# Range check in parts, the copy of an accumulator on two engines, and a new order of convolution products in an attention and convolution kernel

## The chip, the cores and the metric

The kernel runs on one core of a Trainium2 chip. The metric is the time on the device in microseconds (us), from the median of the runs shown. A profile of one execution is given beside it; its span is the stretch between the first and the last recorded instruction, and its own time is a little longer.

In the profile PE is TensorE's matmul stream, PEld its stream of weight loads, DVE is VectorE, ACT is ScalarE, POOL is GpSimd and SP is SyncE, which issues most DMA transfers. An L with a number is a line of the kernel before.

## The reference, cut to what matters

Two layers are computed on `x` of shape (8, 64, 64, 64). The first is attention over the 4096 pixels of each image, with means taken off queries and keys and a second, unary softmax:

```python
sim = jnp.einsum('bcn,bcm->bnm', q - q_mean, k - k_mean) / scale
out = jnp.einsum('bnm,bcm->bcn', jax.nn.softmax(sim, axis=2), v)
unary = jax.nn.softmax(jnp.einsum('bc,bcm->bm', q_mean, k - k_mean), axis=-1)
x = x + out + jnp.einsum('bcm,bm->bc', v, unary)[:, :, None]
```

The second takes signs of `x`, convolves them with binarized weights of sizes 1, 3 and 5 (each followed by a batch norm), sums the three, and gates the sum:

```python
s = sum(qconv_bn(x, move_k, w_k, ...) for k in (1, 3, 5))
gate = jax.nn.sigmoid(grouped_linear(jnp.mean(s, axis=(2, 3))))
return s * gate[:, :, None, None] + x
```

## The kernel before, in words

Two images lie side by side on the 128 partitions, so there are `n_pairs` = 4 pairs. The 4096 pixels of a pair are cut into `NQ` = 8 query blocks of 512 columns: 32 blocks in all, numbered g from 0 to 31. A block has 32 steps j. In each step TensorE makes the scores of 128 keys against 512 queries for both images (`ps`, L474, eight float32 matmuls on quadrants of 64x64), ScalarE takes their exponential (`e`, L485), TensorE multiplies it with the values into the accumulator `acc` (L493, eight matmuls), and VectorE adds `e` into `es` (L508) for the denominators. The scores of step j+1 are issued ahead of the product of step j.

`attend` writes the order of all this out by hand. `plan(g)` says which further work is put behind which step. At step 0 of a block stand:

- `weighted_out` of the block before: ScalarE copies `acc`, 128 x 1024 values in two PSUM banks, into the tile `o` (L515). `added` (L582) later adds the two halves of it on VectorE.
- `send` and `gather`: transfers that re-lay `es` for the division.
- `mix_rows`: convolution products of the block three before (L703, with the 1x1 convolution at L785) and, in front of them, the projections of the queries of the next block (`pq`, L460), which VectorE (L467) and ScalarE (L468) turn into `q`.

Within `mix_rows` two sequences run side by side on the two row halves of TensorE's array. One has the query projections, the ten "S" products of the 5x5 convolution, the 1x1 convolution and the twelve products `three` of the 3x3 convolution (A, B, S and D, three each). The other has the projections and the "A", "B" and "D" products of the 5x5 convolution. Their lengths are given in units and the two are merged by these. When the 1x1 convolution is done, ScalarE's `begin_rows` (L729) reads it. When the twelve 3x3 products are done, ScalarE's `hold_rows` (L734) copies them out as `es_z`. When all is done, VectorE's `add_rows` follows (L744, L750).

PSUM has three pools: `ps_s` with two slots of two banks for the scores and the 5x5 products, `ps_a` with one slot of two banks, and `ps_m` with two single banks. The one slot of `ps_a` is taken in turn by `acc` of a block, by the 3x3 products `z3` of `mix_rows`, and by `acc` of the next block. So the first 3x3 product follows the copy of the old `acc`, and the first matmul of the new `acc` follows `hold_rows`.

A range check guards the result: each reciprocal that the softmax uses must lie between 1e-20 and 1e20. `check` has ScalarE take signs of the value against both limits and add them up into a column of the tile `fit`. At the end VectorE adds `fit` up and compares (L1162, L1163), TensorE sums over the partitions (`pb`, L1165), VectorE casts the count to an integer (`good`, L1167), each engine loads it into a register (L1168), and `tc.If` (L1171) jumps over a slow path that is taken only if a check failed. All that stands after `attend` in the text and is placed by a scheduler.

The tail of `attend`, from L1098, handles the last block. It is cut into 320 and 192 columns (`parts`, `halves`). Its reciprocals are made on VectorE (L576), `finish` (L586, L587), signs on ScalarE (L613, L619), then the last two of three direct convolutions, `mix` of rows 6 to 11 and 11 to 16 (L785, with the results on ScalarE at L805 and on VectorE at L809). Then come the check of all 512 reciprocals (L418), `gate_mean` (L815), `gate` (a matmul L819, an exponential L821, L822, L823), a diagonal matrix of the gate (L1127), and the eight results: two through TensorE (`pre`, L1130), ScalarE's copy (L1131) and ScalarE's DMA queue (L1132), six through VectorE (L827) and SP's queue (L828).

Of the kernel before, what the change touches and what calls it, by code (L numbers as in the profile page):

```python
# [18 lines left out]
F32 = mybir.dt.float32  # L19
BF16 = mybir.dt.bfloat16  # L20
I32 = mybir.dt.int32
AF = mybir.ActivationFunctionType
ALU = mybir.AluOpType
AX = mybir.AxisListType
PSUM = bass.MemoryType.PSUM

P = 128
# [4 lines left out]
QB = 512  # L32
NQ = N // QB
# [11 lines left out]
def conv_seq_kernel(ctx, tc, x, wq, wk, wv, vecs, w1, w3, w5, wtap, gw, out):  # L45
    nc = tc.nc
    n_pairs = x.shape[0] * x.shape[1] // P
# [4 lines left out]
    cp = ctx.enter_context(tc.tile_pool(name="const", bufs=1))  # L52
# [3 lines left out]
    fp = ctx.enter_context(tc.tile_pool(name="fp", bufs=1))  # L56
    sm = ctx.enter_context(tc.tile_pool(name="small", bufs=2))
# [5 lines left out]
    def m_tile(name):  # L63
        return ps_m.tile([P, QB], F32, tag="m", name=name)
# [12 lines left out]
    gw_s = cp.tile([P, P], F32, tag="gw", name="gw_s")  # L77
# [28 lines left out]
    ones = cp.tile([P, P], F32, tag="ones", name="ones")  # L106
# [5 lines left out]

    rec = cp.tile([P, 8], F32, tag="rec", name="rec")

    fit = cp.tile([P, 2, n_pairs * (NQ + 1)], F32, tag="fit", name="fit")
    lim = cp.tile([P, 3], F32, tag="lim", name="lim")
    nc.vector.memset(lim[:, 0:1], -LOW)
    nc.vector.memset(lim[:, 1:2], HIGH)
# [138 lines left out]
    class Pair:  # L257
# [152 lines left out]
        def check(self, r, i, sides=(0, 1)):  # L410

            w = r.shape[-1]
            for side in sides:
                if w < QB:
                    junk = self.tile(sm, "ck", f"{i}_{side}", (P, 8), BF16)
                else:
                    junk = self.tile(fp, "rc", f"ck_{i}_{side}", dtype=BF16)
                nc.scalar.activation(  # L418
                    junk[:, 0:w],
                    r,  # L420
                    AF.Sign,
                    bias=lim[:, side : side + 1],
                    scale=1.0 - 2.0 * side,
                    accum_out=fit[:, side, i : i + 1],
                )
# [84 lines left out]
        def weighted_out(self, qb, parts=(slice(0, QB),)):  # L510

            acc = self.acc[qb]
            self.acc[qb] = self.tile(fp, "o", qb, (P, 2, QB))
            for c in parts:
                nc.scalar.copy(self.acc[qb][:, :, c], acc[:, :, c])  # L515

# [59 lines left out]
        def added(self, qb, cols=slice(0, QB)):  # L578
            if cols.start == 0:
                self.x2[qb] = self.tile(bp, "x2", qb)  # L580
            acc = self.acc[qb]
            nc.vector.tensor_tensor(self.x2[qb][:, cols], acc[:, 0, cols], acc[:, 1, cols], ALU.add)  # L582

        def finish(self, qb, cols=slice(0, QB)):
            x2 = self.x2[qb][:, cols]
# [229 lines left out]
            nc.vector.tensor_reduce(self.ga, self.gap[:, 0 : self.n_gaps], AX.X, ALU.add)  # L815

        def gate(self):
            pg = m_tile(f"pg_{self.name}")
            nc.tensor.matmul(pg[:, 0:1], gw_s, self.ga, start=True, stop=True)  # L819
            self.gt = self.tile(sm, "gt", 0, (P, 1))  # L820
            nc.scalar.activation(self.gt, pg[:, 0:1], AF.Exp, bias=ngb, scale=-1.0 / N)  # L821
            nc.vector.tensor_scalar(self.gt, self.gt, 1.0, None, ALU.add)  # L822
            nc.vector.reciprocal(self.gt, self.gt)  # L823
# [57 lines left out]
    def mix_rows(q, c):  # L881


        seqs = [[], []]
        if q is not None:
            for h in range(2):
                seqs[h].append((("q",), 0, 2.0))
        if c is not None:
            p, (r0, _, y) = c
            qb = r0 // ROWS  # L890

            def products(k, name):
                return [((k, name), i, 0.5) for i in range(n_products(k, name))]

            S = products(5, "S")
            three = [t for name in "ABSD" for t in products(3, name)]
            seqs[0] += S[:8] + [((1,), 0, 1.0)] + three + S[8:]
            seqs[1] += products(5, "A") + products(5, "B") + products(5, "D")
        order = []
        for h, seq in enumerate(seqs):  # L900
            at = 0.0
            for t in seq:
                order += [(at, h, b, t) for b in (h, 1 - h)]
                at += t[2]
        order.sort(key=lambda o: o[0:2])
        if q is not None:
            q[0].query_tiles(q[1])
        z, left = {}, {}
        for o in order:
            left[o[3][0]] = left.get(o[3][0], 0) + 1  # L910
        half = [slice(0, QB // 2), slice(QB // 2, QB)]
        for _, h, b, (n, i, _) in order:
            if n == ("q",):
                q[0].split_queries(q[1], b, h)
            else:
                if n not in z:
                    name = f"{p.name}_{qb}_{n[0]}"
                    if n == (1,):
                        z[n] = m_tile(f"z{name}")
                    elif n == (5, "D"):  # L920
                        z[n] = m_tile(f"z{name}d")[:, half[0]]
                    elif n[0] == 3:
                        z3 = ps_a.tile([P, 2, QB], F32, tag="acc", name=f"z{name}")
                        for j, m in enumerate("ABSD"):
                            z[3, m] = z3[:, j // 2, half[j % 2]]
                    else:
                        t = score_banks(f"z{name}")
                        z[5, "S"], z[5, "A"], z[5, "B"] = t[0][:, half[0]], t[1][:, half[0]], t[1][:, half[1]]
                if n == (1,):
                    p.conv_tap((r0, ROWS, y), [[z[n]]], b, 0, 0, 0, True, True)  # L930
                else:
                    p.row_product(z[n], b, *n, i, r0)
            left[n] -= 1
            if left[n] == 0 and n == ("q",):
                q[0].split_queries_out(q[1])
            elif left[n] == 0 and n == (1,):
                p.begin_rows(qb, z[n])
            elif left[n] == 0 and n == (3, "D"):
                p.hold_rows(qb, z3)
        if c is not None:  # L940
            p.add_rows(qb, z[5, "A"], z[5, "B"], z[5, "S"])
            p.z5d = z[5, "D"]
# [21 lines left out]
    def attend(pairs):  # L964
        pending = None
        n_blocks = n_pairs * NQ
# [114 lines left out]
        for g in range(n_blocks):  # L1081
            pr, qb = divmod(g, NQ)
            at = plan(g)
            p = pairs[pr]
# [13 lines left out]
        p, b = pairs[-1], NQ - 1  # L1098
# [14 lines left out]
        for (r0, r1), cols in zip(parts, halves):  # L1113
            if r0 > 0:
                p.reciprocals_wide(b, slice(cols.start + P, cols.stop))
                p.finish(b, cols)
            for n in (2, 1):
                p.signs_wide(b, n, r0, r1, None)
                p.copy_signs(b, n, r0, r1, (nc.vector.tensor_copy, nc.gpsimd.tensor_copy))
            p.signs(b, r0, r1, nc.gpsimd.tensor_copy)  # L1120
        mix(None, (p, p.joint_rows(6, 11)), one_bank, score_banks)
        mix(None, (p, p.joint_rows(11, 16)), one_bank, score_banks)
        p.check(p.r[b], n_blocks - 1)
        p.gate_mean()
        p.gate()
        diag_g = sm.tile([P, P], F32, tag="diag_g", bufs=1, name="diag_g")
        nc.vector.tensor_scalar(diag_g, ident, p.gt, None, ALU.mult)  # L1127
        rows_p = rows_of(n_pairs - 1)
        for i in range(2):
            nc.tensor.matmul(pre[:, i, :], diag_g, p.s[i], start=False, stop=True)  # L1130
            nc.scalar.copy(p.s[i], pre[:, i, :])  # L1131
            nc.scalar.dma_start(out=of[rows_p, bass.ts(i, QB)], in_=p.s[i])  # L1132
        for i in range(2, NQ):
            p.store(i, rows_p)

    with tc.manual_schedule():
        first = Pair("0", xt)
        warm(6)
        projection()
        warm(4)  # L1140
        first.mean_part(0, quarters[0])
        vectors()
        first.mean_part(1, quarters[1], True)
        first.mean_part(2, quarters[2])
        for c in range(2):
            first.mean_part(3 + c, slice(N * (6 + c) // 8, N * (7 + c) // 8), c == 1)
        first.query_tiles(0, score_banks)
        for b in range(2):
            first.queries(0, b)
        load_weights()  # L1150
        warm(18)
        first.mean_sum(5)
        first.mean_scores()
        first.mean_scores_out()
        first.queries_out(0)
        key_bias()
        first.value_weights()
        attend([first] + [None] * (n_pairs - 1))


    nb_ = sm.tile([P, 1], F32, tag="nb", name="nb")
    nc.vector.tensor_reduce(nb_, fit, AX.XY, ALU.add)  # L1162
    nc.vector.tensor_scalar(nb_, nb_, n_pairs * (16.0 * NQ + 2.0) - 16.0 + 2 * QB, None, ALU.is_equal)  # L1163
    pb = m_tile("pb")
    nc.tensor.matmul(pb[:, 0:1], ones, nb_, start=True, stop=True)  # L1165
    good = sm.tile([P, 1], I32, tag="good", name="good")
    nc.vector.tensor_copy(good, pb[:, 0:1])  # L1167
    n_good = nc.values_load(good[0:1, 0:1])  # L1168


    with tc.If(n_good < P):  # L1171
# [117 lines left out]
```

## Time and profile before

| What | Value |
|---|---|
| Median of 3 runs | 1933.31 us (1933.23 to 1934.18) |
| Profiled execution, its own time | 1934.02 us |
| Its span | 1931.8 us |
| TensorE matmuls busy | 1914.2 us, 99% of the span |
| VectorE busy | 1594.1 us, 83% |
| ScalarE busy | 1274.0 us, 66% |
| TensorE clock granted | 1.0 up to 1922.25 us, 0.5 after it |
| ScalarE's copies of `acc` (L515, 1024 columns) | 31, mean 1006 ns |
| `hold_rows` (L734) | 29, mean 1114 ns |

The page that these come from gives busy times by engine, the chain of work that ended last, and groups of instructions by line with the mean time of one and the idle time before it. An engine at 99% can still lose time: matmuls overlap, so start times of neighbours tell more than the busy share.

### The profile page before, as it was taken

What the parts mean: (1) busy time and instruction counts of PE and PEld (TensorE: products, weight loads), DVE (VectorE), ACT (ScalarE), POOL (GpSimd) and SP (SyncE); (2) the same over time, 40 slices, a digit from 0 to 9 for tenths busy, and PEclk for the clock granted to TensorE, in tenths of its full rate; (3) what the DMA queues carried; (4) which work ended last, traced back from release to release, by engine and by line L of the source; (5) the groups of instructions that cost most, each with busy time, mean ns of one, the idle gap of its engine ahead of it and who ended that gap; (6) DMA issues with size and microseconds to landing.
All of it is one profiled execution on the core that took longest, in us unless ns stands there. A gap on an engine that the chain in (4) does not pass through costs nothing.

```text
span 1931.8 us, 48355 instructions
## 1 busy us (share of the span) xinstructions
PE 1914.2 (99%) x20848; PEld 754.9 (39%) x20848; DVE 1594.1 (83%) x2066; ACT 1274.0 (66%) x1523; POOL 5.9 (0%) x26
## 2 busy tenths in 40 slices
PE   9999999999999999999999999999999999999997
PEld 4333343343333333343433333433443333333334
DVE  6878888889887888888888888898887888877876
ACT  5667766666666766666666676666666666666663
POOL 0000000000000000000000000000000000000000
PEclk9999999999999999999999999999999999999999
DMA  3021110110112110101101211011011011111111
GB/s 101 31 70 29 28 40 32 40 35 16 40 35 80 56 51 27 41 32 40 35 16 40 84 53 57 28 29 40 32 40 35 16 56 50 49 39 37 25 35 46
DMA packets 58998, 80.58 MB, mean 42 GB/s; under 512 B 15628, under 2 KB 40600, under 8 KB 58648
## 3 DMA queue, kind: packets, MB, share of 16 engines
q1 hardware_dynamic: 58024, 76.22, 12.9%
q8 instruction: 165, 2.70, 0.6%
q10 hardware_dynamic: 720, 1.18, 0.2%
q14 instruction: 57, 0.47, 0.1%
q0 software_dynamic: 32, 0.01, 0.0%
HBM read 39.27 MB, written 24.77 MB: 33 GB/s over the span
## 4 chain that ended last, share of the span: by engine, by line
PE 97%; DVE 1%; ACT 1%; DMA 0%; issue 0%; SPq 0%; DVEq 0%
PE ps L474 46%; PE acc L493 45%; PE z L703 4%; PE pv L313 1%; PE pq L460 1%; PE z L785 1%; ACT e L485 0%; DMA x<-in_x 0%; DVE es L508 0%; PE warm L155 0%; DVE r L576 0%; PE z_5d L703 0%; DMA out<-sb 0%; ACT o L515 0%; ACT rc_ck L418 0%
## 5 line engine op out<-in xcount | busy, mean ns | idle before, releaser
L485 ACT ACTIVATE e<-ps 128x1024 f32<-128x1024 f32 x1024 | 1049.7, 1025 | 597.8 <-PE ps L474 576.8
L508 DVE TENSOR_TENSOR es<-es,e 128x1024 f32<-128x1024 f32 x960 | 1171.2, 1220 | 187.6 <-ACT e L485 158.2
L474 PE MATMUL ps<-q,x 64*64 64x512 f32 x8192 | 1069.5, 590 | 0.9 <-DVE kb L165 0.9
L493 PE MATMUL acc<-e,v 64*64 64x512 f32 x8192 | 1065.2, 590 | 0.6 <-ACT e L485 0.3
L493 PEld LDWEIGHTS acc<-e,v 64*64 64x64 f32 x8192 | 307.6, 131 | 577.8 <-ACT e L485 305.9
L474 PEld LDWEIGHTS ps<-q,x 64*64 64x64 f32 x8192 | 312.2, 133 | 528.9 <-issue 278.0
L703 PE MATMUL z<-e,wt 64*64 64x256 bf16 x754 | 69.3, 270 | 0.1
L703 PE MATMUL z<-ec,wt 64*64 64x256 bf16 x754 | 69.4, 270 | 0.0
L744 DVE SCALAR_TENSOR_TENSOR sb<-z,scale,sb 128x256 f32<-128x256 f32 x29 | 14.0, 483 | 65.4 <-PE z L703 62.2
L703 PEld LDWEIGHTS <-wt 64*64 64x64 bf16 x1508 | 65.0, 105 | 0.4 <-issue 0.4
L703 PE MATMUL z<-ec,wc 64*64 64x256 bf16 x464 | 60.5, 270 | 0.0
L506 DVE TENSOR_TENSOR es<-e,e 128x1024 f32<-128x1024 f32 x32 | 39.2, 1225 | 24.5 <-ACT e L485 24.5
L703 PEld LDWEIGHTS <-wc 64*64 64x64 bf16 x1218 | 55.6, 106 | 4.8 <-issue 0.6
L619 ACT ACTIVATE s<-x,vec 128x512 bf16<-128x512 f32 (+2 forms) x66 | 46.1, 702 | 5.2 <-DVE x L587 5.2
L757 DVE TENSOR_TENSOR sb<-sb,es_z 128x256 f32<-128x256 f32 x116 | 43.9, 420 | 1.0
L703 PE MATMUL z<-e,wc 64*64 64x256 bf16 x319 | 44.4, 270 | 0.0
L734 ACT ACTIVATE es_z<-z,frac 128x1024 f32<-128x1024 f32 x29 | 32.3, 1114 | 16.3 <-PE z L703 16.3
L515 ACT COPY o<-acc 128x1024 f32<-128x1024 f32 (+2 forms) x33 | 32.3, 981 | 1.2 <-PE acc L493 1.2
L467 DVE TENSOR_SCALAR q<-pq,mx 128x256 f32<-128x256 f32 x30 | 14.5, 484 | 20.8 <-PE pq L460 20.8
L313 PEld LDWEIGHTS pv<-wx,x 64*64 64x64 f32 x1024 | 21.6, 134 | 17.8 <-issue 9.2
L703 PE MATMUL z<-s,wc 64*64 64x256 bf16 x145 | 25.4, 270 | 0.0
L587 DVE SCALAR_TENSOR_TENSOR x<-x,ou,x 128x512 f32<-128x512 f32 (+2 forms) x33 | 24.3, 735 | 1.2
(156 smaller groups left out, 743.6 us busy)
## 6 DMA issues: line engine op xcount, KB each, us to landing
es<-es SPq DMA_DIRECT2D x31, 512.0 KB
e_parts<-es SPq DMA_DIRECT2D x124, 128.0 KB
r<-rc SPq DMA_DIRECT2D x62, 128.0 KB
x<-in_x SPq DMA_DIRECT2D x15, 512.0 KB
out<-sb SPq DMA_DIRECT2D x28, 256.0 KB
ec<-e SPq DMA_DIRECT2D x29, 153.0 KB
xc<-in_x SPq DMA_DIRECT2D x60, 64.0 KB
ec<-e SPq DMA_DIRECT2D x29, 132.0 KB
```

What stands on the lines that cost most here:

```text
L313: nc.tensor.matmul(pv[img[h], b, i * w : (i + 1) * w], self.x[img[b], bass.ds((4 * g + i) * P + h * H, H)], self.wx[img[b], :], start=True ...
L474: nc.tensor.matmul(ps[img[h], b, :], self.x[img[b], bass.ds(j * P + h * H, H)], self.q[qb][img[b], :], start=True, stop=neg is None,)
L485: nc.scalar.activation(e, ps, AF.Exp, scale=1.0 / 8.0)
L493: nc.tensor.matmul(self.acc[qb][img[b], h, :], self.v[img[h], j, img[b]], e[img[h], b, :], start=(j == 0), stop=(j == NK - 1),)
L506: nc.vector.tensor_tensor(self.es[qb], self.first, e, ALU.add)
L508: nc.vector.tensor_tensor(self.es[qb], self.es[qb], e, ALU.add)
L515: nc.scalar.copy(self.acc[qb][:, :, c], acc[:, :, c])
L587: nc.vector.scalar_tensor_tensor(x2, x2, self.ou, self.x[:, bass.ts(qb, QB)][:, cols], ALU.add, ALU.add)
L619: nc.scalar.activation(sy[n][0][:, rows, pad : pad + HH], self.x2[qb][:, r0 * HH : r1 * HH].rearrange("p (h w) -> p h w", w=HH), AF.Sign, ...
L703: nc.tensor.matmul(z[img[b], :].rearrange("p (h w) -> p h w", w=HH), taps[img[h], c * C : c * C + C], src[:, first : first + 3 * step + 1 ...
L734: nc.scalar.activation(z, two, AF.Identity, scale=frac[3][:, 0:1])
L757: nc.vector.tensor_tensor(out, out, self.z3[i], ALU.subtract if (i, t) == (3, 1) else ALU.add)
```

## The change

It has four parts.

1. `weighted_out` copies the first half of `acc` on ScalarE and the second on VectorE, into two tiles, `o0` and `o1`.
2. In `mix_rows` the first sequence has another order: five S products, six of the 3x3 products, the 1x1 convolution, the other six 3x3 products, then five S products.
3. The check of the last block is made for 320 and for 192 columns, each as soon as its part of the reciprocals is there. The verdict is formed ahead of the last convolution's results, ScalarE casts it, and each engine loads it into its register ahead of the gate and the results.
4. Of the two results that go through TensorE and ScalarE, both products come first, then both copies, then both transfers.

```diff
-    fit = cp.tile([P, 2, n_pairs * (NQ + 1)], F32, tag="fit", name="fit")
+    fit = cp.tile([P, 2, n_pairs * (NQ + 1) + 1], F32, tag="fit", name="fit")
...
-                if w < QB:
+                if w <= 8:
                     junk = self.tile(sm, "ck", f"{i}_{side}", (P, 8), BF16)
...
             acc = self.acc[qb]
-            self.acc[qb] = self.tile(fp, "o", qb, (P, 2, QB))
+            self.acc[qb] = [self.tile(fp, f"o{h}", qb) for h in range(2)]
             for c in parts:
-                nc.scalar.copy(self.acc[qb][:, :, c], acc[:, :, c])
+                nc.scalar.copy(self.acc[qb][0][:, c], acc[:, 0, c])
+                nc.vector.tensor_copy(self.acc[qb][1][:, c], acc[:, 1, c])
...
-            nc.vector.tensor_tensor(self.x2[qb][:, cols], acc[:, 0, cols], acc[:, 1, cols], ALU.add)
+            nc.vector.tensor_tensor(self.x2[qb][:, cols], acc[0][:, cols], acc[1][:, cols], ALU.add)
...
         def gate(self):
-            pg = m_tile(f"pg_{self.name}")
-            nc.tensor.matmul(pg[:, 0:1], gw_s, self.ga, start=True, stop=True)
+            self.gate_logits()
+            self.gate_out()
+
+        def gate_logits(self):
+            self.pg = m_tile(f"pg_{self.name}")
+            nc.tensor.matmul(self.pg[:, 0:1], gw_s, self.ga, start=True, stop=True)
+
+        def gate_out(self):
+            pg = self.pg
...
-            seqs[0] += S[:8] + [((1,), 0, 1.0)] + three + S[8:]
+            seqs[0] += S[:5] + three[:6] + [((1,), 0, 1.0)] + three[6:] + S[5:]
...
             p.signs(b, r0, r1, nc.gpsimd.tensor_copy)
+            if r0 == 0:
+                p.check(p.r[b][:, cols], n_blocks - 1)
         mix(None, (p, p.joint_rows(6, 11)), one_bank, score_banks)
+        p.check(p.r[b][:, halves[1]], n_pairs * (NQ + 1))
+
+        nb = sm.tile([P, 1], F32, tag="nb", name="nb")
+        nc.vector.tensor_reduce(nb, fit, AX.XY, ALU.add)
+        nc.vector.tensor_scalar(
+            nb, nb, n_pairs * (16.0 * NQ + 2.0) - 16.0 + 2 * QB, None, ALU.is_equal
+        )
         mix(None, (p, p.joint_rows(11, 16)), one_bank, score_banks)
-        p.check(p.r[b], n_blocks - 1)
+        pb = m_tile("pb")
+        nc.tensor.matmul(pb[:, 0:1], ones, nb, start=True, stop=True)
+        good = sm.tile([P, 1], I32, tag="good", name="good")
+        nc.scalar.copy(good, pb[:, 0:1])
         p.gate_mean()
-        p.gate()
+        p.gate_logits()
+        n_good = nc.values_load(good[0:1, 0:1])
+        p.gate_out()
...
         for i in range(2):
             nc.tensor.matmul(pre[:, i, :], diag_g, p.s[i], start=False, stop=True)
+        for i in range(2):
             nc.scalar.copy(p.s[i], pre[:, i, :])
+        for i in range(2):
             nc.scalar.dma_start(out=of[rows_p, bass.ts(i, QB)], in_=p.s[i])
...
-    nb_ = sm.tile([P, 1], F32, tag="nb", name="nb")
-    nc.vector.tensor_reduce(nb_, fit, AX.XY, ALU.add)
-    nc.vector.tensor_scalar(nb_, nb_, n_pairs * (16.0 * NQ + 2.0) - 16.0 + 2 * QB, None, ALU.is_equal)
-    pb = m_tile("pb")
-    nc.tensor.matmul(pb[:, 0:1], ones, nb_, start=True, stop=True)
-    good = sm.tile([P, 1], I32, tag="good", name="good")
-    nc.vector.tensor_copy(good, pb[:, 0:1])
-    n_good = nc.values_load(good[0:1, 0:1])
```

More of the change, by code (lines that the diff above doesn't have):

```diff
@@ L1134, in attend @@
             p.store(i, rows_p)
+        return n_good
     with tc.manual_schedule():
@@ L1157, in conv_seq_kernel @@
         first.value_weights()
-        attend([first] + [None] * (n_pairs - 1))
-    nb_ = sm.tile([P, 1], F32, tag="nb", name="nb")
-    nc.vector.tensor_reduce(nb_, fit, AX.XY, ALU.add)
-    nc.vector.tensor_scalar(nb_, nb_, n_pairs * (16.0 * NQ + 2.0) - 16.0 + 2 * QB, None, ALU.is_equal)
-    pb = m_tile("pb")
-    nc.tensor.matmul(pb[:, 0:1], ones, nb_, start=True, stop=True)
-    good = sm.tile([P, 1], I32, tag="good", name="good")
-    nc.vector.tensor_copy(good, pb[:, 0:1])
-    n_good = nc.values_load(good[0:1, 0:1])
+        n_good = attend([first] + [None] * (n_pairs - 1))
     with tc.If(n_good < P):
```

## The prediction

> **What bounds the kernel now.** I read the page first. TensorE is busy for 99% of the span and the chain that ended last is 97% TensorE, so time leaves only where TensorE stands, or from the tail, where other engines set the end. Lines of the page and of the list of waits:
>
> ```profile
> PE 1914.2 (99%) x20848; PEld 754.9 (39%) x20848; DVE 1594.1 (83%) x2066; ACT 1274.0 (66%) x1523; POOL 5.9 (0%) x26
> ...
> PE 97%; DVE 1%; ACT 1%; DMA 0%; issue 0%; SPq 0%; DVEq 0%
> ...
> L744 DVE SCALAR_TENSOR_TENSOR sb<-z,scale,sb 128x256 f32<-128x256 f32 x29 | 14.0, 483 | 65.4 <-PE z L703 62.2
> ```
> ```profile
> PEld acc L493 <- ACT es_z L734: 22.2, 29, 0.9
> ```
>
> The second fence matters most: once in each of 29 blocks the first matmul of `acc` waits for ScalarE's `hold_rows` (L734), since `z3` and `acc` take turns in one PSUM slot. The 22.2 us are idle time of the weight loads, which run ahead; TensorE's own loss is smaller. I took it from the start times of single matmuls around L734. From the second four `ps` matmuls to the next `ps` takes 1.288 us in a steady step. At the block boundary it takes 1.63 us in 23 blocks (0.34 lost in each, 0.36 in the last) and 1.288 in the other six, which place small matmuls ahead of `ps`. So **23 x 0.343 = 7.9 us** are lost in one place. One boundary, in the timeline:
>
> ```profile
> 1016.70 1.01 ACT L515 COPY o<-acc 128x1024 f32<-128x1024 f32 x1
> 1017.07 0.48 DVE L467 TENSOR_SCALAR q<-pq,mx 128x256 f32<-128x256 f32 x1 [0.72 <-PE pq L460]
> ...
> 1018.14 0.78 ACT L729 ACTIVATE sb<-z,shift,scale 128x512 f32<-128x512 f32 x1
> ...
> 1019.47 1.11 ACT L734 ACTIVATE es_z<-z,frac 128x1024 f32<-128x1024 f32 x1 [0.56 <-PE z L703]
> ...
> 1020.64 0.21 PEld L493 LDWEIGHTS acc<-e,v 64*64 64x64 f32 x8 [0.88 <-ACT es_z L734]
> 1020.64 1.09 PE L493 MATMUL acc<-e,v 64*64 64x512 f32 x8
> ```
>
> See that `acc` starts 0.05 after L734 ends, and that L734 started when the last product for `z3` was done. The tail, in the chain of waits:
>
> ```profile
> 1917.23 0.02 issue
> 1917.26 0.24 DVE nb L1162
> 1917.50 0.02 issue
> 1917.52 0.15 DVE nb L1163
> 1917.67 0.47 DVE es_j L809
> ```
> ```profile
> DVE nb L1162 <- ACT rc_ck L418: 0.8, 1, 0.8
> ```
>
> VectorE's last sums (L809) stand behind the verdict's reduction, which stands behind ScalarE's check of 512 columns. Their matmuls ended at 1916.91, so they lose 1917.59 - 1916.97 = 0.6 us.
>
> [...] L467 read PSUM for 0.485 us under the running copy L515, and its mean is 0.484. The two new copies read different banks. [...] SP's branch (L1171) at 1925.90 was followed by its next instruction at 1929.19. [...] In the trace the clock is 1.0 until 1922.25 and 0.5 after it.
>
> **The change, part by part.** Block 17 above serves for all; d is any new TensorE stall ahead of `z3`.
>
> *New order of products.* Nothing is added. A slot of four matmuls takes 0.111 us. Now: eight S slots from 1016.83, the 1x1 (two slots) at 1017.71, `z3` from 1017.93 to 1019.15, L734 0.32 after that last start. New: five S, so `z3` begins at 1017.38; the 1x1 at 1018.05; the last `z3` product at 1018.82+d. L734 could then start at 1019.14+d. ScalarE must first do `begin_rows` (0.78): the 1x1 ends 0.38 after its start, plus 0.04 for the signal, so 1018.47 to 1019.25+d, and successive ScalarE instructions overlap by about 0.09 (copy at 1016.70 under an exponential that ended at 1016.80[...]). L734: 1019.15 to 1020.26+d, `acc` free at 1020.31+d. TensorE reaches it at 1020.35+d (1.17 - 0.88 = 0.29 before 1020.64). So the wait goes, with 0.04 us to spare; late next is `begin_rows`, equal to the `z3` products. I leave e = 0.03 for weights loaded late (the 0.05 by which `acc` lasts longer today, reduced).
>
> *Copy of `acc` by two engines.* `z3` needs the slot 0.55 us earlier than now, so the copy must be shorter. ScalarE: 128x512 from PSUM takes 0.586 (L1131, L321) for 1.01, so 1016.70 to 1017.29; released at 1017.34. VectorE: no row has this copy. PSUM copies of 128 and 192 columns took 0.290 and 0.356 (L160, L227), 1.03 ns a column: 0.69 for 512. [...] the upper bound is 0.743 (L442, 512 columns with a scalar). VectorE is free (its last `es` sum ended 1016.35, `q` starts 1017.07), `acc` ends at 1016.57 and a signal to VectorE takes 0.07: 1016.65 to 1017.34, release 0.05 later, 1017.39. `z3` wants 1017.38. So **d is 0.01 by these numbers; I take 0.05**, for a second wait on TensorE (such an instruction lasts 0.051) and lost lead of weight loads. Bounds: 0 if the slot is held only by ScalarE's half, 0.2 if VectorE is slow and both extras add. Behind VectorE's copy stands `q`: it ends at about 1017.75 and its bank is wanted by the 1x1 at 1018.05, so nothing waits; the queries are of the next block. Then VectorE idles until 1019.77 (the 62.2 us in L744's row are this gap), which hides 31 x 0.69 = 21 us of new work. If that cover were gone, `add_rows` would be late, not TensorE. `added` reads two tiles in place of one, at the same cost.
>
> Sum: 22 x (0.343 - 0.05 - 0.03) = 5.8. Six blocks without a stall pay d: -0.3. In the last block, which has no `pq`, `z3` waits for the copies now (0.27) and would wait from an earlier slot: some 0.2 remain of its 0.36. **5.7 us.**
>
> *Tail.* (a) VectorE copies 320 and 192 columns (0.49 + 0.36) ahead of `added`, which waited until 1905.39 anyway: it starts near 1905.6, the reciprocals at 1906.1 for 1905.89: **+0.2** (0.1 to 0.4). (b) Check of the first 320 columns: two activations and accumulator reads, 2 x 0.67, in ScalarE's idle 1.68 us before L619; if that cover went, L619 would be late by the rest. The other 192 columns: 2 x 0.57 between the two L805, where ScalarE idles 1.04: L805 up to 0.1 late, which VectorE, busy until 1915.85 and then with the verdict's 0.4 us, doesn't see. The last sums no longer wait: **-0.6**. (c) The verdict's matmul and cast (0.36, about 0.26) run while VectorE still sums. The register loads (0.49 to 1.07 by the L1168 rows) start near 1917.8 and stand ahead of ScalarE's exponential (wanted at 1919.05), TensorE's `diag_g` product and VectorE's gate: all hidden, ScalarE's by 0.1 to 0.2; uncovered they would cost up to 0.6. SP and POOL load while they wait. (d) Both `diag_g` products in a row (1.98 for four such instructions, L1105) and two copies end at 1923.2, where the second copy ended at 1924.98: -1.8 on ScalarE; its two issues of 0.36 follow, and its register load of 1.07 is gone from the end. But SP's six stores, each behind 0.66 us of VectorE, start with the gate and load all 16 DMA engines until 1929.5; the end follows the last landing by fixed steps. So (c) and (d) are hidden by the stores, and the tail moves with the gate: **-0.4**, from +0.3 (loads uncovered) to -1.4 [...].
>
> Total -6.1. Against the profiled execution (span 1931.8, own time 1934.02) that is a span of 1925.7 and 1927.9. The three runs have a median of 1933.31, 0.71 below it, so I forecast **1927.2**.
>
> **Rivals.**
> 1. *The copy is late* (d = 0.15 to 0.2, e = 0.05): 23 x 0.12 - 1.2 + 0.4 = 2 us gained, **1931.3**: no change. For it: 0.01 us of room, two signals in place of one. Against: LDWEIGHTS already sits ahead of the wait.
> 2. *VectorE's copy becomes the bound, slower.* It frees `z3`'s slot in all 29 blocks. Gain and loss balance at d = 7.9/29 = 0.27; at 0.45, **1938**: 29 x 0.45 - 7.9 = 5.2 lost, less the tail. That needs a copy of 1.1 us, or a start held 0.4 by the queue. Against: 0.743 at most, and VectorE free 0.3 earlier in every one of the 29 blocks.
> 3. *The reorder does not do what it says*: `begin_rows` comes later than I place it and L734 stays, or the copies stay late; only the tail moves: **1932.9**.
>
> **How the numbers follow.** A difference below 0.2% (3.9 us) can't be told from none. Forecast 0.66 (1924.5 to 1929.4, from d = 0, e = 0 with tail -1.2, to d = 0.11); rival 1 0.15; rival 2 0.11; rival 3 0.08. The first is faster nearly always, 1 and 3 are no change. The range 1924.5 to 1932.9 leaves out rival 2 and some of the ends.
>
> **What would show it.** Right: the wait of `acc` for `es_z` falls from 22.2 us to below 8, a `ps` step at the boundary takes 1.29 to 1.35, VectorE has 31 copies of 0.66 to 0.75 us, and the gap ahead of L744 shrinks by them; in the tail nothing lies between the first of the last three sums and its matmuls. Wrong: a new wait of `z` for the copy over 0.27 a block, copies near 1 us, or an unchanged 0.34 at `acc`.

## The result: 0.9% slower, and the profile after

| | before | after |
|---|---|---|
| Median of 4 runs each | 1933.74 us (1933.23 to 1934.77) | 1950.38 us (1949.83 to 1952.03) |
| Profiled execution, own time | 1934.02 us | 1949.83 us |
| Its span | 1931.8 us | 1947.7 us |

The ratio is 1.0087, with a 95% interval of 1.0069 to 1.0104. The forecast was 1927.2 us, with a range up to 1932.9, and a loss had a chance of 0.11. So the forecast was wrong in sign, by 23 us.

The page after shows the loss without naming it. The first line has busy times by engine; the second has the shares of the chain that ended last; the others are groups of instructions (busy us, mean ns of one, then the idle time ahead of the engine and what ended it):

```profile
PE 1914.8 (98%) x20848; PEld 896.7 (46%) x20848; DVE 1612.0 (83%) x2098; ACT 1258.0 (65%) x1528; POOL 5.9 (0%) x26
...
PE 94%; ACT 3%; DVE 2%; DMA 0%; issue 0%; SPq 0%; DVEq 0%
...
L704 PE MATMUL z<-e,wt 64*64 64x256 bf16 x754 | 74.8, 271 | 14.9 <-DVE o L516 14.9
...
L745 DVE SCALAR_TENSOR_TENSOR sb<-z,scale,sb 128x256 f32<-128x256 f32 x29 | 14.0, 484 | 60.3 <-PE z L704 54.2
...
L516 DVE COPY o<-acc 128x512 f32<-128x512 f32 (+2 forms) x33 | 22.3, 676 | 29.8 <-ACT o L515 29.8
```

TensorE's busy time rose by only 0.6 us while the span rose by 15.9. Its share of the last chain fell from 97% to 94%, and ScalarE and VectorE took those 3%. The convolution products of `z` (L704) now stand for 14.9 us behind VectorE's copy (L516), which in turn stands for 29.8 us behind ScalarE's copy (L515). The list of waits gives the counts (us in total, times, longest):

```profile
DVE o L516 <- ACT o L515: 29.8, 32, 1.0
...
PE z L704 <- DVE o L516: 14.9, 29, 0.9
...
PEld acc L493 <- ACT es_z L735: 13.6, 26, 0.6
```

VectorE's copy waits for ScalarE's in 32 of 33 cases, and TensorE pays in all 29 blocks that have 3x3 products. One boundary, in ScalarE's timeline and then VectorE's (start, duration):

```profile
1023.51 1.02 ACT L485 ACTIVATE e<-ps 128x1024 f32<-128x1024 f32 x1 [0.69 <-PE ps L474]
1024.43 0.58 ACT L515 COPY o<-acc 128x512 f32<-128x512 f32 x1
1024.89 0.49 ACT L468 ACTIVATE q<-pq,nmx 128x256 f32<-128x256 f32 x1
1026.90 0.78 ACT L730 ACTIVATE sb<-z,shift,scale 128x512 f32<-128x512 f32 x1 [1.52 <-PE z L786]
1027.58 1.10 ACT L735 ACTIVATE es_z<-z,frac 128x1024 f32<-128x1024 f32 x1
```
```profile
1025.04 0.69 DVE L516 COPY o<-acc 128x512 f32<-128x512 f32 x1 [0.97 <-ACT o L515]
1025.65 0.48 DVE L467 TENSOR_SCALAR q<-pq,mx 128x256 f32<-128x256 f32 x1
```

VectorE was idle for 0.97 us, yet its copy starts 0.03 us after ScalarE's has ended. The two lie end to end: 1024.43 to 1025.01, then 1025.04 to 1025.73. The chain of work at this boundary shows the price:

```profile
1024.53 0.48 ACT o L515
1025.02 0.02 issue
1025.04 0.70 DVE o L516
1025.74 0.04 issue
1025.79 0.86 PE z L704 x21
```

The last S products started at 1025.0. The first of `z3`, whose weights were loaded from 1025.00 on, would have followed 0.11 us later, and comes at 1025.79. On the mean this new stall, the d of the prediction, is **0.68 us**, where 0.05 was taken.

Matmuls overlap (before, the first four `acc` matmuls of a block start within 0.02 us and one lasts 0.59), so from the start times of single matmuls I summed the stretches of TensorE's work. A group of four matmuls is timed by the start of its first. The boundary is the time from a block's last four `acc` matmuls to the next block's first.

| Stretch, sums in us | before | after |
|---|---|---|
| Block boundaries | 144.23 | 158.51 |
| Steps 1 to 31 of all blocks | 1672.53 | 1673.78 |
| First to second step of `acc`, blocks 1 to 31 | 54.38 | 54.14 |
| Last `acc` matmul to the end | 27.78 | 28.32 |

The four differences are +14.3, +1.25, -0.24 and +0.54, together 15.8 of the 15.9 us by which the span is longer. A boundary without other small work took 4.67 and takes 5.06 to 5.17; the six that had no stall before, and could only lose, grew by 0.70 to 0.80.

### The profile page after: what moved, and what is told of

It reads as the page before. It is cut to its first block, busy times and chain, and to the rows that moved or that the text cites. A ratio compares the mean times of both kernels' runs of the same rounds, so it can differ in the third digit from the quotient of the medians.

```text
span 1947.7 us, 48398 instructions
## 1 busy us (share of the span) xinstructions
PE 1914.8 (98%) x20848; PEld 896.7 (46%) x20848; DVE 1612.0 (83%) x2098; ACT 1258.0 (65%) x1528; POOL 5.9 (0%) x26
## 4 chain that ended last, share of the span: by engine, by line
PE 94%; ACT 3%; DVE 2%; DMA 0%; issue 0%; SPq 0%; DVEq 0%
PE ps L474 45%; PE acc L493 43%; PE z L704 3%; ACT e L485 2%; DVE o L516 1%; ACT o L515 1%; PE z L786 1%; PE pv L313 1%; DMA x<-in_x 0%; PE warm L155 0%; DVE es L508 0%; DVE r L577 0%; DVE sb L835 0%; PE z_5d L704 0%; DVE es_j L835 0%
## 5 line engine op out<-in xcount | busy, mean ns | idle before, releaser
L474 PE MATMUL ps<-q,x 64*64 64x512 f32 x8192 | 1115.7, 590 | 0.9 <-DVE kb L165 0.9
L493 PE MATMUL acc<-e,v 64*64 64x512 f32 x8192 | 1113.0, 589 | 0.6 <-ACT e L485 0.3
L474 PEld LDWEIGHTS ps<-q,x 64*64 64x64 f32 x8192 | 399.8, 133 | 441.7 <-issue 222.9
L493 PEld LDWEIGHTS acc<-e,v 64*64 64x64 f32 x8192 | 355.8, 131 | 524.4 <-ACT e L485 307.9
L704 PE MATMUL z<-e,wt 64*64 64x256 bf16 x754 | 74.8, 271 | 14.9 <-DVE o L516 14.9
L704 PE MATMUL z<-ec,wt 64*64 64x256 bf16 x754 | 74.7, 272 | 0.0
L704 PEld LDWEIGHTS <-wt 64*64 64x64 bf16 x1508 | 63.1, 105 | 21.2 <-issue 21.2
L704 PE MATMUL z<-ec,wc 64*64 64x256 bf16 x464 | 60.5, 270 | 0.0
L704 PEld LDWEIGHTS <-wc 64*64 64x64 bf16 x1218 | 57.0, 106 | 3.3 <-issue 0.4
L730 ACT ACTIVATE sb<-z,shift,scale 128x512 f32<-128x512 f32 x29 | 22.6, 778 | 44.4 <-PE z L786 44.4
L516 DVE COPY o<-acc 128x512 f32<-128x512 f32 (+2 forms) x33 | 22.3, 676 | 29.8 <-ACT o L515 29.8
L704 PE MATMUL z<-e,wc 64*64 64x256 bf16 x319 | 44.5, 270 | 0.0
L313 PEld LDWEIGHTS pv<-wx,x 64*64 64x64 f32 x1024 | 23.4, 134 | 16.1 <-issue 8.3
L321 ACT COPY v<-pv 128x512 f32<-128x512 f32 x32 | 18.8, 586 | 9.3 <-PE pv L313 9.2
```

What stands on the lines that cost most here:

```text
L313: nc.tensor.matmul(pv[img[h], b, i * w : (i + 1) * w], self.x[img[b], bass.ds((4 * g + i) * P + h * H, H)], self.wx[img[b], :], start=True ...
L474: nc.tensor.matmul(ps[img[h], b, :], self.x[img[b], bass.ds(j * P + h * H, H)], self.q[qb][img[b], :], start=True, stop=neg is None,)
L493: nc.tensor.matmul(self.acc[qb][img[b], h, :], self.v[img[h], j, img[b]], e[img[h], b, :], start=(j == 0), stop=(j == NK - 1),)
L516: nc.vector.tensor_copy(self.acc[qb][1][:, c], acc[:, 1, c])
L704: nc.tensor.matmul(z[img[b], :].rearrange("p (h w) -> p h w", w=HH), taps[img[h], c * C : c * C + C], src[:, first : first + 3 * step + 1 ...
```

## The experiments

My theory after the result: the new order does its work, and all of the loss comes from the VectorE copy, since it stands behind ScalarE's, both reading one tile of PSUM. The main rival: the new order is itself the harm, because it wants the slot earlier than any copy can give it back. A third question was where the tail's gain had gone. Medians of before beside these runs were 1933.94 (first four) and 1933.91 us (last four). The last three columns are sums over the profiled execution of each kernel.

| Kernel | Median, us | Ratio to before, 95% | Boundaries | Steps | Tail |
|---|---|---|---|---|---|
| e1: new order, one copy | 1940.31 | 1.0032 (1.0020 to 1.0044) | 149.69 | 1673.81 | 27.66 |
| e2: old order, two engines | 1939.53 | 1.0028 (1.0017 to 1.0039) | 148.76 | 1672.56 | 28.66 |
| e3: new order, two engines, two tiles | 1929.97 | 0.9980 (0.9974 to 0.9987) | 139.72 | 1674.08 | 27.35 |
| e4: new tail alone | 1934.06 | 1.0003 (0.9995 to 1.0012) | as before | as before | 27.51 |
| e5: e3 with the old order | 1932.67 | 0.9993 (0.9985 to 1.0002) | 141.57 | 1674.14 | 27.69 |
| e6: e3, both parts of `hold_rows` late | 1931.48 | 0.9988 (0.9981 to 0.9995) | 139.73 | 1674.73 | 27.24 |
| e7: e5, ScalarE alone copies | 1929.15 | 0.9975 (0.9965 to 0.9985) | 137.58 | 1674.15 | 27.85 |
| e8: e7 with the old tail | 1928.82 | 0.9974 (0.9965 to 0.9984) | 137.57 | 1674.12 | 28.11 |

### e1: the new order, with one copy on ScalarE

Against the kernel after:

```diff
-                nc.scalar.copy(self.acc[qb][0][:, c], acc[:, 0, c])
-                nc.vector.tensor_copy(self.acc[qb][1][:, c], acc[:, 1, c])
+                nc.scalar.copy(self.acc[qb][:, :, c], acc[:, :, c])
```

> The changed kernel, but ScalarE copies all 1024 columns of acc again, as before; the new order of products and the new tail stay. Theory A (VectorE's copy waits for ScalarE's, so the slot of z3 is freed at 0.58 + 0.69 us after acc ends, too late for products that now want it 0.55 us earlier): one copy of 1.01 us frees the slot 0.31 us earlier than the two in a row. z3 waits about 0.38 us instead of 0.68 in each of 29 blocks, the 0.34 us at acc stay gone in 23. About 1937 us (1935 to 1940), between the two kernels. Rival B (the new order itself makes TensorE slow, by weight loads or by the accumulation banks, whoever copies): 1945 or more, with no less than 0.6 us lost per block ahead of z3.

1940.31 us (1939.96 to 1942.89). Taking VectorE's copy away wins back 10.1 of the 16.6 us. From its list of waits:

```profile
PEld acc L493 <- ACT es_z L734: 13.6, 26, 0.6
...
PE z L703 <- ACT o L515: 6.2, 29, 0.6
```

The wait of `z` for VectorE is gone, and one for ScalarE's copy of 1.01 us is in its place: `z3` starts 0.47 us after the product ahead of it, 0.38 later than it could have, the 0.38 that I had expected. So the new order by itself costs more with the old copy (0.38 in 29 blocks) than the 0.343 that it saves in 23, as both theories say. The median is 0.3 us over the range that I gave: the steps lost 1.3 us, which I had not counted. The profiled execution took 1942.89 us; most of what it has over the median lies ahead of the first `acc` matmul (19.9 us after the start, 17.3 before), and so in none of the three columns.

### e2: the two copies, with the old order

```diff
-            seqs[0] += S[:5] + three[:6] + [((1,), 0, 1.0)] + three[6:] + S[5:]
+            seqs[0] += S[:8] + [((1,), 0, 1.0)] + three + S[8:]
```

> The changed kernel with the old order of products; the two copies of acc, on ScalarE and VectorE, and the new tail stay. Theory A: VectorE's copy still starts after ScalarE's, the slot is free 0.30 us later than before, and z3, which had 0.17 us to spare, waits 0.12 us in 29 blocks (3.6 us); acc still loses 0.34 us in 23 blocks; the tail is 0.5 us longer. About 1938 us (1936 to 1940). Rival B (the new order is the harm): about the time of before, 1933 to 1935, and no wait of z3 for a copy.

1939.53 us (1939.32 to 1940.15), within the range. From its waits:

```profile
DVE o L516 <- ACT o L515: 29.8, 32, 1.0
...
PEld acc L493 <- ACT es_z L735: 22.5, 29, 0.9
```

The wait between the copies is the same 29.8 us as after, to the digit: it does not come from the order of the products. `z3` starts 0.12 us later than before, as I had expected, in place of 0.68, since the old order asks for the slot later. The old wait at `acc` stays at 22.5. The rival falls as the whole cause: without the new order the kernel is still slower than before. But neither is my theory the whole. The two copies without the new order cost 5.6 us (e2), the new order without them 6.4 (e1), and both together 16.6, all three with the new tail: the copies free the slot later while the order asks for it sooner.

### e3: each half of the slot a tile of its own

Here each of `acc`, `z3` and the tail's `pre` is two tiles of one bank in place of one tile of two; the banks are the same in number. `hold_rows` becomes two instructions of 512 columns, the first as soon as the products A and B are done. Order, engines and tail are those of after.

```diff
+    def acc_tiles(name):
+        return [ps_a.tile([P, QB], F32, tag=f"acc{h}", name=f"{name}_{h}") for h in range(2)]
...
-                self.acc[qb] = ps_a.tile([P, 2, QB], F32, tag="acc", name=f"acc_{self.name}_{qb}")
+                self.acc[qb] = acc_tiles(f"acc_{self.name}_{qb}")
...
-            nc.scalar.activation(z, two, AF.Identity, scale=frac[3][:, 0:1])
+            nc.scalar.activation(z[:, i, :], two[i], AF.Identity, scale=frac[3][:, 0:1])
...
+            elif left[n] == 0 and n == (3, "B"):
+                p.hold_rows(qb, z3, 0)
```

> The changed kernel with each half of acc in a PSUM tile of its own (one bank each), and z3 and the diagonal products likewise; hold_rows is two activations of 512 columns, the first as soon as the A and B products are done. Theory A (what ties the two copies together is that both read one tile): VectorE's copy starts with ScalarE's, within 0.1 us, z3 doesn't wait, acc doesn't wait. 1925 to 1927 us. Rival B (the new order is the harm) 1935 or more. Rival C (the two engines can't read PSUM side by side, whatever the tiles): VectorE's copy starts after ScalarE's or lasts over 1 us, and the time stays above 1940.

1929.97 us (1929.17 to 1932.37), ratio 0.998 (0.9974 to 0.9987): faster than before, 20.4 us faster than after. A boundary in ScalarE's timeline and in VectorE's:

```profile
1017.06 0.58 ACT L518 COPY o<-acc 128x512 f32<-128x512 f32 x1
```
```profile
1017.02 0.69 DVE L519 COPY o<-acc 128x512 f32<-128x512 f32 x1 [0.32 <-PE acc L496]
```

The copies now run side by side, with the durations that they had end to end (0.58 and 0.69). VectorE's starts first and is released by the last `acc` matmul, no longer by ScalarE. This is the overlap that the prediction had assumed. TensorE waits for a copy ahead of `z3` in one block only, for 0.2 us; a boundary without other work takes 4.38 to 4.50 us in place of 4.67.

It was 3 us short of the 1925 to 1927 expected. In the profiled execution, which took 1931.08 us, 2.3 us were lost in one place: 1.1 at the boundary of block 1 and 1.2 in its first step. A table by stretches of the first blocks (length, busy us by engine, the granted clock, DMA) of e3 and of the kernel before:

```profile
70.00:78.20 8.20, 6.79 (x68) 2.70 (x64) 7.26 (x15) 4.62 (x7) 0.00 (x0) 1.00 0.15 59
78.20:81.60 3.40, 3.40 (x20) 1.05 (x16) 1.12 (x2) 1.60 (x5) 0.00 (x0) 0.50 0.40 120
```
```profile
70.00:78.20 8.20, 7.39 (x76) 2.89 (x72) 6.57 (x13) 5.41 (x11) 0.00 (x0) 1.00 0.17 66
78.20:81.60 3.40, 3.40 (x36) 1.22 (x32) 1.85 (x2) 2.05 (x2) 0.00 (x0) 1.00 0.42 126
```

In 78.20 to 81.60 TensorE is busy throughout in both, but at half clock in e3, with 20 matmuls for 36. Ahead of that stretch it had stood idle for longer. In the timeline of TensorE, e3 and then before:

```profile
77.26 0.38 PE L366 MATMUL po<-ones,vu 128*128 128x1 f32 x2 [1.41 <-DVE q L470]
```
```profile
76.45 0.38 PE L363 MATMUL po<-ones,vu 128*128 128x1 f32 x2 [0.81 <-DVE q L467]
```

In block 1 there is no convolution work to cover the boundary, and VectorE's copy stands ahead of its `q` (L470), for which TensorE waits. (Block 2 has none either; its boundary took 3.27 us for 3.07.) The idle of 1.41 us in e3 was followed by clock 0.50, that of 0.81 before by clock 1.00. e5 and e6 have an idle of 1.4 there as well, and e7 and e8, in which VectorE copies nothing, one of 0.8. But before, an idle of 1.39 us up to 6.54 was not followed by half clock: the clock is 1.0 from 3.96 to 1922.25. So half clock doesn't follow from the length of the idle alone. That it was there in other executions of e3 isn't shown, so the 2.3 us can't be taken off the median.

### e4: the new tail alone

The middle is that of before, with the tail of after and one ScalarE copy for each part.

```diff
+            if r0 == 0:
+                p.check(p.r[b][:, cols], n_blocks - 1)
...
+        p.check(p.r[b][:, halves[1]], n_pairs * (NQ + 1))
...
+        p.gate_logits()
+        n_good = nc.values_load(good[0:1, 0:1])
+        p.gate_out()
```

> The kernel before with the changed tail alone: the check in parts, the verdict and the register loads ahead of the results, ScalarE's two results together; the old order of products and one copy of acc on ScalarE. By the prediction's steps the last sums start 0.6 us sooner and the end follows the gate: 1933.1 us. If the second diagonal product at half clock and the stores set the end, as they seem to do in the changed kernel, the gain is given back: 1933.5 to 1934.

1934.06 us (1933.36 to 1936.66), ratio 1.0003: no change that this measurement can tell. The tail's steps are in its chain of work:

```profile
1915.03 2.86 PE z L785 x61
1917.89 0.03 issue
1917.92 0.56 DVE es_j L809
...
1920.48 0.30 DVE diag_g L1148
1920.78 0.04 issue
1920.82 3.61 PE pre L1151 x4
```

VectorE's last sums (L809) follow their matmuls after 0.03 us, with no verdict between. The gate's product `pre` starts 15.85 us after the last `acc` matmul, against 16.47 before: 0.6 gained, as priced. Then the four products in a row take 3.61 us, where the prediction had 1.98. Before, two of these took 1.12 us at clock 1.0 and the other two 2.08 at 0.5; an estimate from these is that most of the four ran at half clock in e4. The end comes only 0.27 us earlier than in the profile of before.

### e5: two tiles, two engines, the old order

The edit is that of e3 with the order line of e2.

> Two PSUM tiles, one copy on each engine at the same time and hold_rows in two parts, as in the run before, but with the old order of products. Theory A: z3 doesn't wait for the copies; but VectorE's copy puts the queries q back to about 0.05 us after the old place of the 1x1 convolution, which takes over their bank, so the 1x1 waits some 0.1 us in 29 blocks. hold_rows in two parts ends 0.4 us sooner, so acc doesn't wait in spite of the old order. 1928 to 1931 us, the same as with the new order within 0.1%. Rival (the new order of products is what frees acc): the 0.34 us at acc come back in 23 blocks, 1934 or more.

1932.67 us (1931.51 to 1933.88), ratio 0.9993 (0.9985 to 1.0002): not told from no change. TensorE's wait at `acc` is gone here too, so the two tiles with the two-part `hold_rows` remove it in the old order, and the rival that it returns falls. What is left is a 1x1 convolution that starts 0.09 us late (the expected wait was 0.1): its bank is freed by VectorE's `q`, which stands behind VectorE's copy. With copies that do run side by side the new order is worth 1932.67 - 1929.97 = 2.7 us, though the two ran beside different runs of before; their boundaries differ by 1.85.

### e6: two tiles, `hold_rows` in two instructions, both at the end

Against e3:

```diff
-            elif left[n] == 0 and n == (3, "B"):
-                p.hold_rows(qb, z3, 0)
...
+                p.hold_rows(qb, z3, 0)
                 p.hold_rows(qb, z3, 1)
```

> Two PSUM tiles, parallel copies, new order; the two parts of hold_rows are both issued after the D products. Theory A: no wait of z3, but the second part ends 1.3 us after the D products where one activation took 1.1, so acc waits 0.15 us in 23 blocks: about 3.4 us over the kernel with the first part early, 1931 to 1934. Rival (parallel copies are the whole of that kernel's gain, the part put early adds nothing): 1929 to 1931.

1931.48 us (1930.25 to 1936.49). This is the kernel after with nothing changed but the tiles (and `hold_rows` as two instructions in its old place), and it takes 18.9 us less: 29 blocks x 0.65 us. The boundaries alone have 18.8 less. From its waits:

```profile
DVE o L519 <- PE acc L496: 9.6, 30, 0.3
```

VectorE's copy is released by the matmuls again, as in e3. **So the shared tile carries the whole of d.** Two tiles bring two things, copies side by side and a slot that is handed over in halves; in the new order they were not tested apart.

Of e3's gain, the early first half of `hold_rows` is worth 1.5 us by the medians, where I had expected 3.4. Its place is not the one of my theory: the boundaries of e3 and e6 agree (139.72 and 139.73), so the first `acc` matmul of a block doesn't come later in e6. The last of its four does, by 0.05 in most blocks. What differs in the sums are the steps, by 0.65, and the first step of block 1, by 0.4. With intervals of 0.0014 the size is not settled.

### e7: two tiles, ScalarE copies both halves, the old order

Against e5:

```diff
-                nc.vector.tensor_copy(self.acc[qb][1][:, c], acc[1][:, c])
+                nc.scalar.copy(self.acc[qb][1][:, c], acc[1][:, c])
```

> Two PSUM tiles and hold_rows in two parts with the first early, old order, new tail, and both halves of acc copied by ScalarE in two instructions of 512 columns. Theory A: the first bank is free 0.58 us after acc ends, ahead of A and B, the second 0.49 later, ahead of S and D, so z3 doesn't wait; q stays where it was before the change, so the 1x1 doesn't wait; acc doesn't wait, since the second part of hold_rows is only 0.69 us. All of the 7.9 us at acc are gained: 1926 us (1925 to 1928). Rival (the second engine is needed to free the slot): a wait of 0.2 us or more ahead of z3 in 29 blocks, 1930 or more.

1929.15 us (1927.41 to 1931.28). Its ScalarE timeline at one boundary:

```profile
1014.54 0.58 ACT L518 COPY o<-acc 128x512 f32<-128x512 f32 x1
1015.01 0.60 ACT L519 COPY o<-acc 128x512 f32<-128x512 f32 x1
...
1016.66 1.34 ACT L739 ACTIVATE es_z<-z,frac 128x512 f32<-128x512 f32 x2
```

Two copies in a row take 1.07 us for the 1.01 of one. In the old order nothing waits for the second, and each half of the slot is free by itself: 137.58 us of boundaries for 144.23, 6.65 gained where 7.9 were expected. The mechanism was right. The median is above the 1925 to 1928 given, since the steps took 1.6 us back; why they do stands at the end of the next section.

### e8: the same with the old tail

The edit is the kernel before with the two tiles, two copies on ScalarE and the two-part `hold_rows`, and nothing else.

> The kernel before with two PSUM tiles, ScalarE's copy of acc in two instructions and hold_rows in two parts; order of products and tail as before. Theory A: the same middle as with the new tail, so 1926 to 1927 us; the new tail is worth 0 to 0.4 us.

1928.82 us (1928.34 to 1931.63), ratio 0.9974 (0.9965 to 0.9984): 5.1 us faster than before, 21.6 faster than after. The new tail adds nothing that e7 and e8 can tell. Neither the second engine, nor the new order, nor the new tail is needed for this gain. The halved copy and the halved `hold_rows` were not tested apart.

## Why the prediction was wrong, step by step

**What bounds the kernel: the right place, sized too high.** TensorE did lose time at `acc`, and e7 and e8 gain 6.65 us at the boundaries. But 1.6 of these come back as loss inside the blocks. The 7.9 us were read from the first of four matmuls, and the last of the four loses less; see the last paragraph of this section.

**The new order: right.** After, the wait of the weight loads at `acc` fell from 22.2 to 13.6 us (below 8 was forecast), and the next `ps` comes 1.32 to 1.33 us after the second four `ps` matmuls in the 23 blocks where it took 1.63 (1.29 to 1.35 was forecast). So e, taken as 0.03, measured 0.04. In e3, without the stall at `z3`, the remaining wait is 4.7.

**The copy on two engines: the step that failed.** The words are "VectorE is free (...), `acc` ends at 1016.57 and a signal to VectorE takes 0.07: 1016.65 to 1017.34". Both durations were right (0.58 and 0.69 measured for 0.586 and 0.69). The start was wrong: I priced the resources, an idle engine and a free bank, and did not ask what the second instruction must wait for. In e3 the two copies, each of a bank of its own, start at 1017.02 and 1017.06 and last 0.69 and 0.58 us, as long as they took one after the other. But that the hardware ran them at once there does not mean that the program lets it: after, with the two banks in one tile, the second copy starts when the first has ended. The term in the sum was d = 0.05, with 0.2 as its upper bound. It measured 0.68: VectorE's copy was placed 0.05 ahead of ScalarE's start and came 0.03 after its end, 0.66 later, and the prediction's own times had left 0.01. The sum with it is 22 x (0.343 - 0.68 - 0.03) = -8.1, six blocks at -0.68 = -4.1, and the last block's further 0.6: 12.8 us lost. The boundaries lost 14.3; for the other 1.5 I have no term.

The table of before held no instance of two engines reading one tile at one time: L467 under L515, which I quoted as evidence, reads another tile. The bounds that the prediction set (0 to 0.2) spanned durations alone. The lower bound of the overlap, none at all, would have given d = 0.65 to 0.7 and a loss of over 10 us.

**Rival 2 named the place and the sign, not the cause.** It had VectorE's copy as the bound of `z3`'s slot, a break-even at d = 0.27, and "a start held 0.4 by the queue". The start was held by 0.66 and not by VectorE's queue, which had been idle for 0.97 us, but by ScalarE's copy. I argued against it by VectorE being free, which says nothing of a wait that the program sets.

**The tail: -0.4 forecast, +0.54 measured.** Step (a) was mis-sized: the tail's four copies stand end to end as well, as the chain of work after shows:

```profile
1920.03 0.43 ACT o L515
1920.46 0.02 issue
1920.49 0.50 DVE o L516
1920.99 0.02 issue
1921.01 0.33 ACT o L515
1921.34 0.02 issue
1921.36 0.36 DVE o L516
```

The sum `added` ends 2.75 us after the last `acc` matmul, 1.87 before, and the reciprocals follow it directly in both: +0.8 for the forecast 0.2. Step (b) was right: -0.6, shown alone in e4. The loads of (c) are hidden, as said. Step (d) held that the stores hide the products. These were priced at 1.98 us from a stretch at full clock; after, they took 2.77, with clock 0.5 from 1937.06, in the third of them, and 3.6 in e4. Gate to end took 11.7 us for 11.3. The 16 DMA engines, which the prediction has loaded until 1929.5, were busy before for 0.95 of 1921.5 to 1927.2 and for 0.13 of 1928 to 1929.5. From SP's last semaphore instruction of `tc.If` to the end of the span it is 1.5 us in both (1930.31 to 1931.78, and 1946.22 to 1947.69). SP's branch was followed by its next instruction after 3.29 us before and 4.45 after; what fills that time no run shows, so the forecast's far end of -1.4 was a guess. In e4 and e7 the chain that ended last goes through these products; after and in e8 it goes through VectorE's last results, so that the products cost the 0.4 after is not shown. Together +0.8, -0.6 and +0.4.

**The steps: not in the sum.** Steps 1 to 31 lost 1.25 us after. e1, e3, e5, e6, e7 and e8, all without TensorE's stall at `acc`, lost 1.3 to 2.2; e2 and e4, which keep it, lost nothing. The start times of single matmuls show where it goes. At the boundary ahead of block 17, the four matmuls of a group started as follows, in us from the first of the second four `ps`:

| Group | before | after | e8 |
|---|---|---|---|
| Second four `ps` | 0.00 0.01 0.12 0.14 | 0.00 0.02 0.15 0.15 | 0.00 0.01 0.12 0.14 |
| First four `acc` | 0.72 0.73 0.74 0.74 | 0.43 0.45 0.57 0.58 | 0.43 0.44 0.55 0.57 |
| Next `ps` | 1.63 1.64 1.64 1.65 | 1.32 1.34 1.43 1.44 | 1.29 1.30 1.41 1.42 |

Two of the four run ahead when the convolution products end, in before too. There the stall made all four wait for one release, and they went on together. Without the stall the lead stays. By the first, the boundary is 0.34 us shorter in e8; by the last, 0.23. In twelve blocks the projections `pv` (L313) or the product `pg` (L819) of the gate stand behind step 12. There the four are within 0.02 us again, and just there the step takes longer by the lead: 0.09 to 0.11 in each of the twelve after, 0.15 to 0.17 in e6, where the lead was larger (0.18), and 0.18 in the three `pg` blocks of e8 (0.20). With some 0.1 in the last block these make up the loss. So no step got slower for its own sake: part of the gain at the boundary was the lead of one matmul, and the prediction's 0.343 had counted it.

## What to carry to other kernels

Before pricing two engines on one buffer, ask two questions apart: can the hardware run them at once, and does the program let it. Where no row of the profile shows two readers of one tile overlapping, bound the overlap by none at all; here two tiles in place of one, in as many banks, were worth 19 us. When a buffer passes in turn between users, look first at handing it over in parts on the engine that does it now: that gave the whole gain here (5.1 us in e8), with no second engine and no new order. And read a loss at a wait from the last of the matmuls that run side by side: the first was 0.11 us too high here.

## What the runs showed of the hardware that I had not expected

- **A short idle was followed by half clock, but not always.** In e3, 1.41 us without a TensorE instruction at block 1 were followed by 3.4 us at clock 0.50 (78.20 to 81.60), beginning 0.9 us after work had resumed. Before, 0.81 us in the same place were not, nor 1.39 us up to 6.54. After 2.16 us up to 1919.07 the clock stayed at 1.0 for another 3.2 us, to 1922.25. A length of idle that brings half clock doesn't follow from these runs.
- **Splitting a PSUM copy on ScalarE is nearly free.** Two copies of 512 columns took 1.07 us from first start to last end (e7), one of 1024 took 1.01, since the second starts 0.1 us before the first ends. This was seen at this size only (128 partitions, float32).
- **Matmuls on the four quadrants keep a lead for a whole block.** The four `acc` matmuls of a group start within 0.02 us of each other before. After, in 23 of 32 blocks, the last starts 0.15 to 0.17 us behind the first in the block's first group and 0.10 to 0.13 from the second on, up to step 12 or 13, to step 27 (the last block) or to the end of the block.
